# Reordering the small engines' work in a fused attention kernel that TensorE bounds

## The chip, the cores and the metric

The kernel runs on one core of a Trainium2 chip. The metric is the device time of one execution in microseconds. A core has five engines that run side by side, each working through its own queue: TensorE (PE in the profile, matrix products, with its weight loads as PEld), VectorE (DVE), ScalarE (ACT), GpSimd (POOL) and SyncE (SP). The last three also issue transfers (DMA). Matrix products are accumulated in PSUM[...] and are carried from there to SBUF by VectorE or ScalarE.

## The reference

A self-attention block on 16 images of 512 channels and 32 x 32 = 1024 positions, all in float32, with 4 heads of 128 channels:

```python
xg = x.reshape(b, 8, -1)
mu, var = mean(xg), var(xg)                       # group norm, 8 groups
xn = ((xg - mu) * rsqrt(var + 1e-5)).reshape(b, c, h, w) * gamma + beta
qkv = einsum('oc,bchw->bohw', qkv_w, xn) + qkv_b
q, k, v = to_heads(split(qkv, 3, axis=1))
attn = softmax(einsum('bhnd,bhmd->bhnm', q, k) * 128**-0.5)
out = einsum('bhnm,bhmd->bhnd', attn, v)
out = einsum('oc,bchw->bohw', proj_w, out) + proj_b
return x + out
```

## The kernel before

The kernel goes through the images b and the heads h of each, and in each head through eight steps j, one for each 128 key positions. A step has two halves of 512 query positions. In a half there are one score matmul `s`, the exponential `p` of it on ScalarE, and the weighted-sum matmul `po` of the step before. Between these, the other work of neighbouring images is laid in as "units": in head 0 the second half of the queries and keys (`qk`) of this image; in head 1 the output projection (`pp`) of the image before, and loading, statistics and normalisation of the next image; in head 2 the first half of `qk` of the next image; in head 3 its values (`v`).

```python
def scores(s, half):
    b, h, j = where(s)
    sc = ps_s.tile([P, HALF], F32, tag="s", name=f"s_{s}_{half}")        # two PSUM banks
    nc.tensor.matmul(sc, ks[b, h][:, ts(j, P)], qs[b, h][:, ts(half, HALF)], start=True, stop=True)
    ...
    nc.scalar.activation(ps[s][:, ts(half, HALF)], sc, AF.Exp, scale=SCALE)
    ...                                     # tot (a sum over the steps) on VectorE
```

Each 512 x 512 projection is done by Strassen's scheme with Winograd's sums, on two levels: seven outer products of seven inner ones. Outer sums of the right-hand side (`xt2`, `xt3`, `xt4`, and `t1` in place, in the profile the lines with L277) and inner sums (`qk_t`, `v_t`, `pp_t`, L518) are made on VectorE. One Strassen group keeps two PSUM banks, x and y. Products that share a bank are accumulated on top of each other, so a bank has to be copied out (`p1`, `u2`, `u3`) between two of them:

```python
def kept_copy(n):
    t[n] = upool.tile([P, HALF], F32, tag=n, bufs=1 if n == "u3" else 2, name=f"{name}_{n}")
    nc.scalar.copy(t[n][:, :width], t["x"][:, :width])                   # L448

def p1(): t["x"] = bank("x"); mm(t["x"], 1, True); kept_copy("p1")
def p2(): t["y"] = bank("y"); mm(t["y"], 2, True); out_("c11", t["y"], t["p1"])
def p6(): mm(t["x"], 6, False); kept_copy("u2")
def p5(): t["y"] = bank("y"); mm(t["y"], 5, True)
def p7(): mm(t["x"], 7, False); kept_copy("u3"); out_("c22", t["y"], t["u3"])
def p4(): mm(t["x"], 4, False); out_("c21", t["x"])
def p3(): mm(t["y"], 3, False); out_("c12", t["y"], t["u2"])
# out_: nc.scalar.copy (L565), or nc.vector.tensor_add (L567: qk_r, v_r, pp_r)
```

The sums over the keys (the denominators l) are made per head on VectorE from `tot`, and their reciprocals are written to a row in DRAM and read back, broadcast to all partitions, by two transfers that ScalarE's queue issues. A head's `po` is multiplied by them later (`divide`, L877).

```python
def denominators(b, h):
    tt = lpool.tile([P, N // BLK, BLK], F32, tag="tt", name=f"tt_{b}_{h}")
    nc.vector.transpose(tt.rearrange("p c m -> p (c m)"), t)             # L794
    nc.vector.tensor_reduce(part, tt, AX.X, ALU.add)                     # L796
    ...                                     # a few 32 x 32 operations, then reciprocal r
def spread_inverse(b, h, step):
    if step == 0: nc.scalar.dma_start(row..., inverse.pop((b, h)))       # L816
    else: nc.scalar.dma_start(rinv[b, h], rows_of.pop((b, h)).to_broadcast((P, N)))  # L821
```

The projection of the outputs adds to x again in tiles `y`, of which there are four buffers: each is loaded from x, has the product added (L752, L755), and is stored.

The order in which instructions stand on each engine comes from the framework's scheduler, which works from the program's order and from priorities; the loop is this:

```python
if 0 < s < steps and s % NB == 0:
    denominators(*where(s - 1)[:2])
for half in range(NH2):
    if s < steps:
        scores(s, half)
        if j == 1 and s > NB:
            spread_inverse(*where(s - NB)[:2], half)
        if half == 1 and j == 4 and s > NB:
            with tc.issue_after(added[b, h, 4].ins):
                divide(*where(s - NB)[:2])
    if s > 0:
        weighted_sum(s - 1, half)
    ...                                     # half of this step's units
```

Of the kernel before, what the change touches and what calls it, by code (L numbers as in the profile page):

```python
# [16 lines left out]
P = 128  # L17
# [5 lines left out]


LIMIT = 1e20


class Norm:
# [124 lines left out]
KC = 2  # L153
# [6 lines left out]
def fast_path(ctx, tc, x, sources, out, consts, flag, dims):  # L160
# [70 lines left out]
    def stats_chunk(b, c):  # L231
        if c == 0:
            mvs[b] = gn.tile([P, NCC, 2], F32, tag="mv", name=f"mv_{b}")
        if b == 0:
            norm.chunk(mvs[b], xs[b, c], c)
            return

        junk = lpool.tile([P, N], F32, tag="tt", name=f"junk_{b}_{c}")
        sums = gn.tile([P, 3], F32, tag="st", name=f"sums_{b}_{c}")
        nc.scalar.activation(junk, xs[b, c], AF.Identity, accum_out=sums[:, 0:1])  # L240
        nc.scalar.mul(mvs[b][:, c, 0:1], sums[:, 0:1], 1.0 / N)
        nc.scalar.mul(sums[:, 1:2], sums[:, 0:1], -1.0 / N)
        nc.scalar.activation(
            junk, xs[b, c], AF.Square, bias=sums[:, 1:2], accum_out=sums[:, 2:3]
        )
        nc.scalar.mul(mvs[b][:, c, 1:2], sums[:, 2:3], 1.0 / N)

    def stats_group(b):
        mu, sc = norm.group(mvs.pop(b))
# [20 lines left out]
            ]  # L270
        return b

    def sums_of_b(b, rows=(1, 2), chunks=range(KC)):

        def sub(o, i, j):
            for k in chunks:
                nc.vector.tensor_sub(b[o][k], b[i][k], b[j][k])  # L277

        if 1 in rows:
            sub("t1", "b12", "b11")  # L280
        if 2 in rows:
            sub("t2", "b22", "t1")
            sub("t3", "t2", "b11")
            sub("t4", "b21", "t2")

    def x_sums(b, rows=(1, 2)):
        if 1 in rows:
            xb[b] = halves([xs[b, c] for c in range(NCC)], "x")
        sums_of_b(xb[b], rows)
# [146 lines left out]
    def strassen(name, mm, out_, width=HALF):  # L436


        t = {}

        def bank(which):
            return ps_a.tile([P, HALF], F32, tag=which, name=f"{name}_{which}")

        def kept_copy(n):
            t[n] = upool.tile(
                [P, HALF], F32, tag=n, bufs=1 if n == "u3" else 2, name=f"{name}_{n}"
            )
            nc.scalar.copy(t[n][:, :width], t["x"][:, :width])  # L448
# [24 lines left out]
        def p4():  # L473
            mm(t["x"], 4, False)
            out_("c21", t["x"])

        def p3():
            mm(t["y"], 3, False)
            out_("c12", t["y"], t["u2"])

        units = {1: p1, 2: p2, 3: p3, 4: p4, 5: p5, 6: p6, 7: p7}
        return [units[i] for i in ORDER]

    def two_levels(name, site, b, blocks, finish, sums="make", homes="BBBB", prepare=None):
# [39 lines left out]
        def group_units(g):  # L524
            group = OUTER[g]
            n = len(group)
            have = haves[g]

            def weights():
                have["w"] = group_weights(site, g, b == 0 and site in range(PAIRS))  # L530

            def load(m):
                h = homes.find(homes[g], g + 1)
                if sums == "load" and h > 0:
                    nc.sync.dma_start(sum_tile(h, m), inner_kept[b, h, m])

            def inner_sum(m):
                if sums != "load" and m not in have:
                    make_sum(g, m)

            def inner(i, m):
                return inner_block(g, i, m)

            def mm(acc, j, first):
                an, bn = FACTORS[j]
                t, slot = SLOTS[an]
                for i in range(n):
                    nc.tensor.matmul(  # L548
                        acc[:, ts(i, Q)], have["w"][t][:, i, slot, :], inner(i, bn),
                        start=(first and i == 0), stop=True, skip_group_check=True,  # L550
                    )

            def out_(which, a, c=None):
                row, half = int(which[1]) - 1, int(which[2]) - 1
                if g not in R:
                    R[g] = rpool.tile(
                        [P, 2, 2, HALF], F32, tag=f"r{g % 3}", name=f"{name}_r{g}"
                    )
                dst = R[g][:, :n, row, ts(half, Q)]

                def view(t):
                    return t[:, : n * Q].rearrange("p (i q) -> p i q", q=Q)

                if c is None:
                    nc.scalar.copy(dst, view(a))  # L565
                else:
                    nc.vector.tensor_add(dst, view(a), view(c))  # L567
# [191 lines left out]


    ps, tot, po, rinv, last_eviction = {}, {}, {}, {}, {}
    inverse, rows_of, added = {}, {}, {}
    steps = B * HEADS * NB

    def where(s):
# [3 lines left out]
    def scores(s, half):  # L769
        b, h, j = where(s)  # L770
        sc = ps_s.tile([P, HALF], F32, tag="s", name=f"s_{s}_{half}")
        nc.tensor.matmul(  # L772
            sc, ks[b, h][:, ts(j, P)], qs[b, h][:, ts(half, HALF)], start=True, stop=True
        )
        if half == 0:
            ps[s] = ppool.tile([P, N], F32, tag="p", name=f"p_{s}")
        nc.scalar.activation(ps[s][:, ts(half, HALF)], sc, AF.Exp, scale=SCALE)  # L777
# [164 lines left out]
    def last_projection(b):  # L942
# [29 lines left out]
        sums_of_b(bl, (2,), (1,))  # L972
# [35 lines left out]
    def plan_head(b, h):  # L1008
# [9 lines left out]
        elif h == 1:  # L1018
# [4 lines left out]
            else:  # L1023
# [3 lines left out]
                for r in range(2):  # L1027
# [11 lines left out]
        elif b + 1 == B:  # L1039
# [3 lines left out]
            else:  # L1043
                os_[b, h] = opool.tile([P, N], F32, tag="o", name=f"o_{b}_{h}")
                plan[3].append(lambda: o_blocks(b))
                plan[3].append(lambda: sums_of_b(ob[b], (1,)))
                plan[5].append(lambda: sums_of_b(ob[b], (2,), (0,)))
# [42 lines left out]
    for s in range(steps + 1):  # L1090
        units = []
        if s < steps:
# [4 lines left out]
            if j == NB - 1 and h == 2 and b + 1 < B:  # L1097
                next_v.append(v_groups(b + 1))
                next_qk.append(qk_groups(b + 1, 1))
                units.append(ahead[f"v_{b + 1}"])  # L1100
        if 0 < s < steps and s % NB == 0:
            denominators(*where(s - 1)[:2])
        for half in range(NH2):
            if s < steps:
                scores(s, half)
                if j == 1 and s > NB:
                    spread_inverse(*where(s - NB)[:2], half)
                if half == 1 and j == 4 and s > NB:

                    with tc.issue_after(added[b, h, 4].ins):  # L1110
# [141 lines left out]
```

## Time and profile before

The time is 3247.06 us, the median of three runs (3245.63 to 3248.78). The profiled execution spanned 3251.7 us at a granted TensorE clock of 0.999. Groups of instructions that matter here, from the profile's groups (busy time is a union, the mean is that of one instruction):

| engine and line | what | count | mean, ns |
|---|---|---|---|
| TensorE L772 | score matmul s | 2048 records, two to a matmul | 594 |
| TensorE L548 | projection matmuls, 128 x 256 | 6076 records, two to a matmul | about 380 |
| ScalarE L777 | exponential p, 128 x 512 | 1024 | 596 |
| ScalarE L448 | copies p1, u2, u3 of qk, 128 x 512 | 288 | 585 |
| ScalarE L82 | normalise x, 128 x 512 | 124 | 807 |
| ScalarE L240, L243 | statistics, 128 x 1024 | 60 each | 1051, 1148 |
| ScalarE L241, L242, L246 | statistics, 128 x 1 | 60 each | 204, 190, 194 |
| VectorE L785 | tot, 128 x 1024 | 385 | 1222 |

A line of the timeline reads: start in us, duration in us, engine, source line, operation, output and inputs by the program's names, shapes, count; in brackets the time that the engine was idle before it and what ended the wait. TensorE's matmuls overlap, so what one costs is read from the distance between starts.

### The profile page before, as it was taken

The page shows a single profiled execution, that of the slowest core. Times are in us where ns is not written, and L with a number is a line of the kernel's source. Part 1 is how long each engine was busy: PE and PEld are TensorE (multiplying, and loading weights), DVE is VectorE, ACT ScalarE, POOL GpSimd, SP SyncE. Part 2 cuts the span into 40 slices and gives each one's busy share as a digit, 9 for nine tenths or more (in the row PEclk, how much of TensorE's full clock was granted, in tenths as well). Part 3 has the DMA queues.
Part 4 walks back from the last instruction along what each step waited for, and adds up shares of the span by engine and source line. Part 5 has one row for each costly group of instructions (what it writes and reads, how often), then busy time and mean ns, then how long its engine had stood idle before and what let it go on. Part 6 is the DMA issues. An engine that isn't in the chain of part 4 may idle for free.

```text
span 3251.7 us, 34056 instructions
## 1 busy us (share of the span) xinstructions
PE 3185.4 (98%) x10474; PEld 2178.0 (67%) x10474; DVE 2633.3 (81%) x4625; ACT 1439.8 (44%) x2709; POOL 516.3 (16%) x922
## 2 busy tenths in 40 slices
PE   8999999999999999999999999999999999999999
PEld 6566666766666766667666666666666666666664
DVE  8868878788787888878788787987879878788784
ACT  2534435354353543535435354353534535344442
POOL 0011121111211112111121111212012120121100
PEclk9999999999999999999999999999999999999999
DMA  5555553545545455454554545545455453555531
GB/s 161 186 192 164 180 172 123 186 153 182 172 142 181 145 194 161 161 161 146 187 162 162 169 132 193 164 165 167 136 180 171 164 173 134 182 160 172 181 124 40
DMA packets 209388, 526.92 MB, mean 162 GB/s; under 512 B 32816, under 2 KB 65840, under 8 KB 209200
## 3 DMA queue, kind: packets, MB, share of 16 engines
q1 hardware_dynamic: 128992, 276.88, 27.5%
q0 software_dynamic: 66240, 212.39, 19.5%
q10 hardware_dynamic: 13968, 35.41, 3.4%
q8 instruction: 86, 1.41, 0.2%
q14 instruction: 102, 0.84, 0.1%
HBM read 389.56 MB, written 135.00 MB: 161 GB/s over the span
## 4 chain that ended last, share of the span: by engine, by line
PE 47%; issue 27%; DVE 16%; DMA 7%; POOL 2%; ACT 1%; ACTq 0%; POOLq 0%; SPq 0%; DVEq 0%
PE po L867 13%; PE s L772 13%; PE qk_x L548 6%; PE qk_y L548 5%; PE pp_x L548 4%; DVE qk_t L518 3%; PE pp_y L548 3%; DMA vd<-vu 2%; DVE xt L277 2%; DMA out_y<-y 2%; DMA y<-in_x 2%; DMA v<-vd 1%; DVE qk_r L567 1%; DVE vu L703 1%; DVE tot L785 1%
## 5 line engine op out<-in xcount | busy, mean ns | idle before, releaser
L772 PE MATMUL s<-qk,qk 128*128 128x512 f32 x2048 | 1049.0, 594 | 4.5 <-ACT p L777 4.3
L867 PE MATMUL po<-p,v 128*128 128x512 f32 x2048 | 1053.2, 596 | 0.0
L777 ACT ACTIVATE p<-s 128x512 f32<-128x512 f32 x1024 | 610.0, 596 | 895.9 <-PE s L772 817.1
L867 PEld LDWEIGHTS po<-p,v 128*128 128x128 f32 x2048 | 602.0, 303 | 319.1 <-issue 202.3
L785 DVE TENSOR_TENSOR tot<-tot,p 128x1024 f32<-128x1024 f32 x385 | 470.4, 1222 | 147.9 <-ACT p L777 146.2
L772 PEld LDWEIGHTS s<-qk,qk 128*128 128x128 f32 x2048 | 387.0, 190 | 114.1 <-issue 43.5
L548 PE MATMUL qk_x<-qk_t,w 128*128 128x256 f32 x1344 | 356.8, 384 | 9.4 <-DVE qk_t L518 3.5
L548 PEld LDWEIGHTS qk_x<-qk_t,w 128*128 128x128 f32 x1344 | 250.2, 190 | 170.0 <-issue 66.2
L448 ACT COPY qk_u<-qk_x 128x512 f32<-128x512 f32 (+1 forms) x256 | 136.1, 532 | 262.2 <-PE qk_x L548 208.3
L711 POOL DMA_DIRECT2D vd<-vu x120 | 66.3, 552 | 992.4 <-DVE vu L703 990.7
L567 DVE TENSOR_TENSOR qk_r<-qk_y,qk_u 128x512 f32<-128x512 f32 (+1 forms) x256 | 158.3, 619 | 40.1 <-ACT qk_u L448 26.3
L548 PE MATMUL pp_x<-pp_t,w_proj 128*128 128x256 f32 x630 | 170.8, 388 | 6.7 <-ACT pp_p L448 6.7
L567 DVE TENSOR_TENSOR v_r<-v_y,v_u 128x512 f32<-128x512 f32 (+1 forms) x120 | 76.5, 638 | 112.2 <-ACT v_u L448 82.0
L548 PE MATMUL v_x<-v_t,w_v 128*128 128x256 f32 x630 | 166.7, 381 | 0.0
L522 POOL DMA_DIRECT2D kept_t<-qk_t x240 | 129.2, 540 | 233.4 <-DVE qk_t L518 188.7
L756 POOL DMA_DIRECT2D out_y<-y x120 | 66.2, 552 | 627.4 <-DVE y L755 595.2
L548 PEld LDWEIGHTS pp_x<-pp_t,w_proj 128*128 128x128 f32 x630 | 114.0, 190 | 76.4 <-issue 22.5
L548 PEld LDWEIGHTS v_x<-v_t,w_v 128*128 128x128 f32 x630 | 118.6, 190 | 55.2 <-issue 19.1
L716 POOL DMA_DIRECT2D v<-vd x240 | 140.0, 590 | 83.8 <-issue 60.0
L548 PE MATMUL qk_y<-x,w 128*128 128x256 f32 x512 | 143.5, 382 | 0.0
L448 ACT COPY v_u<-v_x 128x512 f32<-128x512 f32 (+1 forms) x124 | 66.2, 534 | 164.8 <-PE v_x L548 125.0
L646 DVE SCALAR_TENSOR_TENSOR qk<-qk_r,qkb_sb,qk_r 128x512 f32<-128x512 f32 x192 | 137.3, 743 | 1.6
(204 smaller groups left out, 4486.0 us busy)
## 6 DMA issues: line engine op xcount, KB each, us to landing
w<-kept SPq DMA_DIRECT2D x90, 512.0 KB, 4.1
kept_t<-qk_t POOLq DMA_DIRECT2D x180, 256.0 KB, 4.4
v_t<-kept_t SPq DMA_DIRECT2D x180, 256.0 KB, 3.0
w<-kept SPq DMA_DIRECT2D x90, 384.0 KB, 3.9
rinv<-row ACTq DMA_DIRECT2D x63, 512.0 KB, 5.4
x<-in_x POOLq DMA_DIRECT2D x60, 512.0 KB, 5.0
vd<-vu POOLq DMA_DIRECT2D x120, 256.0 KB, 3.4
v<-vd POOLq DMA_DIRECT2D x240, 128.0 KB, 4.6
```

The source lines that it names most:

```text
L448: nc.scalar.copy(t[n][:, :width], t["x"][:, :width])
L518: nc.vector.tensor_sub(to[:, i, :], inner_block(g, i, a), inner_block(g, i, c))
L522: nc.gpsimd.dma_start(t, to)
L548: nc.tensor.matmul(acc[:, ts(i, Q)], have["w"][t][:, i, slot, :], inner(i, bn), start=(first and i == 0), stop=True, skip_group_check=True,)
L567: nc.vector.tensor_add(dst, view(a), view(c))
L646: nc.vector.scalar_tensor_tensor(st[b, h][:, ts(half, HALF)], a, qkb_sb[:, i : i + 1], c, ALU.add, ALU.add)
L711: nc.gpsimd.dma_start(rows[which][ts(h, P), :], u)
L716: nc.gpsimd.dma_start(vs[b, pair][ts(q, BLK), half].rearrange("m h (k i) j -> m (h k) (i j)", k=n), rows[which].rearrange("(k m) (q e) -> ...
L772: nc.tensor.matmul(sc, ks[b, h][:, ts(j, P)], qs[b, h][:, ts(half, HALF)], start=True, stop=True)
L777: nc.scalar.activation(ps[s][:, ts(half, HALF)], sc, AF.Exp, scale=SCALE)
L785: added[b, h, j] = nc.vector.tensor_add(tot[b, h][:, i], tot[b, h][:, i], ps[s][:, i])
L867: nc.tensor.matmul(po[b, h][:, i], v_block(b, h, j), ps[s][:, i], start=(j == 0), stop=(j == NB - 1),)
```

## The change

Five things are changed, all of them in what the small engines do and when:

- The exponentials, the copies that empty PSUM banks, and the additions that do so (`out_`) are put under a raised scheduler priority, so that they are placed ahead of work that can wait.
- The two transfers of a head's reciprocals are issued behind the exponentials of the second halves of steps 1 and 2 (before: both in step 1).
- The outer sums of the next image are made near their use: t1 in head 1, xt2 at the start of head 2, xt3 and xt4 one step later (before: all in head 1). For the last image's outputs the split into rows 2 and 3 keeps the order as it was.
- The sums l of a head are made one step later, so that the transpose and the reduction don't stand at the head's start.
- The statistics of images 1 to 15 on ScalarE work on halves of 512 columns, with two more short operations that add the halves' sums.

```diff
+URGENT = 40
 ...
-        junk = lpool.tile([P, N], F32, tag="tt", name=f"junk_{b}_{c}")
-        sums = gn.tile([P, 3], F32, tag="st", name=f"sums_{b}_{c}")
-        nc.scalar.activation(junk, xs[b, c], AF.Identity, accum_out=sums[:, 0:1])
-        nc.scalar.mul(mvs[b][:, c, 0:1], sums[:, 0:1], 1.0 / N)
-        nc.scalar.mul(sums[:, 1:2], sums[:, 0:1], -1.0 / N)
+        def both(i, func, **kw):
+            for h in range(NH2):
+                junk = lpool.tile([P, HALF], F32, tag="tt", name=f"junk_{b}_{c}_{i}_{h}")
+                nc.scalar.activation(
+                    junk, xs[b, c][:, ts(h, HALF)], func, accum_out=sums[:, 2 * i + h][:, None], **kw)
+        both(0, AF.Identity)
         nc.scalar.activation(
-            junk, xs[b, c], AF.Square, bias=sums[:, 1:2], accum_out=sums[:, 2:3]
+            mvs[b][:, c, 0:1], sums[:, 0:1], AF.Identity, bias=sums[:, 1:2]
         )
-        nc.scalar.mul(mvs[b][:, c, 1:2], sums[:, 2:3], 1.0 / N)
+        nc.scalar.mul(neg, mvs[b][:, c, 0:1], -1.0 / N)
+        nc.scalar.mul(mvs[b][:, c, 0:1], mvs[b][:, c, 0:1], 1.0 / N)
+        both(1, AF.Square, bias=neg)
+        nc.scalar.activation(mvs[b][:, c, 1:2], sums[:, 2:3], AF.Identity, bias=sums[:, 3:4])
+        nc.scalar.mul(mvs[b][:, c, 1:2], mvs[b][:, c, 1:2], 1.0 / N)
 ...                                        # kept_copy
-            nc.scalar.copy(t[n][:, :width], t["x"][:, :width])
+            with tc.high_priority(URGENT):
+                nc.scalar.copy(t[n][:, :width], t["x"][:, :width])
 ...                                        # out_
-                if c is None:
-                    nc.scalar.copy(dst, view(a))
-                else:
-                    nc.vector.tensor_add(dst, view(a), view(c))
+                with tc.high_priority(URGENT):
+                    if c is None:
+                        nc.scalar.copy(dst, view(a))
+                    else:
+                        nc.vector.tensor_add(dst, view(a), view(c))
 ...                                        # scores
-        nc.scalar.activation(ps[s][:, ts(half, HALF)], sc, AF.Exp, scale=SCALE)
+        with tc.high_priority(URGENT):
+            exps[s] = nc.scalar.activation(ps[s][:, ts(half, HALF)], sc, AF.Exp, scale=SCALE)
 ...                                        # head 1, then head 2
-                    plan[6 + r].append(lambda r=r: x_sums(b + 1, (r + 1,)))
+                plan[6].append(lambda: x_sums(b + 1, (1,)))
 ...
+            plan[0].insert(2, lambda: x_sums(b + 1, (2,)))
+            plan[1].append(lambda: x_sums(b + 1, (3,)))
 ...                                        # the loop
-        if 0 < s < steps and s % NB == 0:
-            denominators(*where(s - 1)[:2])
+        if NB < s < steps and s % NB == 1:
+            denominators(*where(s - 2)[:2])
 ...
-                if j == 1 and s > NB:
-                    spread_inverse(*where(s - NB)[:2], half)
+                if j in (1, 2) and half == 1 and s > NB:
+                    with tc.issue_after(exps[s].ins):
+                        spread_inverse(*where(s - NB)[:2], j - 1)
```

More of the change, by code (lines that the diff above doesn't have):

```diff
@@ L236, in stats_chunk @@
             return
-        junk = lpool.tile([P, N], F32, tag="tt", name=f"junk_{b}_{c}")
-        sums = gn.tile([P, 3], F32, tag="st", name=f"sums_{b}_{c}")
-        nc.scalar.activation(junk, xs[b, c], AF.Identity, accum_out=sums[:, 0:1])
-        nc.scalar.mul(mvs[b][:, c, 0:1], sums[:, 0:1], 1.0 / N)
-        nc.scalar.mul(sums[:, 1:2], sums[:, 0:1], -1.0 / N)
+        sums = gn.tile([P, 2 * NH2 + 1], F32, tag="st", name=f"sums_{b}_{c}")
+        neg = sums[:, 2 * NH2 :]
+        def both(i, func, **kw):
+            for h in range(NH2):
+                junk = lpool.tile([P, HALF], F32, tag="tt", name=f"junk_{b}_{c}_{i}_{h}")
+                nc.scalar.activation(
+                    junk, xs[b, c][:, ts(h, HALF)], func, accum_out=sums[:, 2 * i + h][:, None],
+                    **kw,
+                )
+        both(0, AF.Identity)
         nc.scalar.activation(
-            junk, xs[b, c], AF.Square, bias=sums[:, 1:2], accum_out=sums[:, 2:3]
+            mvs[b][:, c, 0:1], sums[:, 0:1], AF.Identity, bias=sums[:, 1:2]
         )
-        nc.scalar.mul(mvs[b][:, c, 1:2], sums[:, 2:3], 1.0 / N)
+        nc.scalar.mul(neg, mvs[b][:, c, 0:1], -1.0 / N)
+        nc.scalar.mul(mvs[b][:, c, 0:1], mvs[b][:, c, 0:1], 1.0 / N)
+        both(1, AF.Square, bias=neg)
+        nc.scalar.activation(
+            mvs[b][:, c, 1:2], sums[:, 2:3], AF.Identity, bias=sums[:, 3:4],
+        )
+        nc.scalar.mul(mvs[b][:, c, 1:2], mvs[b][:, c, 1:2], 1.0 / N)
     def stats_group(b):
@@ L271, in halves, with sums_of_b @@
         return b
-    def sums_of_b(b, rows=(1, 2), chunks=range(KC)):
+    def sums_of_b(b, rows=(1, 2, 3), chunks=range(KC)):
         def sub(o, i, j):
@@ L282, in sums_of_b, with x_sums @@
             sub("t2", "b22", "t1")
+        if 3 in rows:
             sub("t3", "t2", "b11")
             sub("t4", "b21", "t2")
-    def x_sums(b, rows=(1, 2)):
+    def x_sums(b, rows=(1, 2, 3)):
         if 1 in rows:
@@ L761, in fast_path @@
     ps, tot, po, rinv, last_eviction = {}, {}, {}, {}, {}
-    inverse, rows_of, added = {}, {}, {}
+    inverse, rows_of, added, exps = {}, {}, {}, {}
     steps = B * HEADS * NB
@@ L971, in last_projection @@
         l, recip = last_division(b, HEADS - 1)
-        sums_of_b(bl, (2,), (1,))
+        sums_of_b(bl, (2, 3), (1,))
         for r in range(2):
@@ L1046, in plan_head @@
                 plan[3].append(lambda: sums_of_b(ob[b], (1,)))
-                plan[5].append(lambda: sums_of_b(ob[b], (2,), (0,)))
+                plan[5].append(lambda: sums_of_b(ob[b], (2, 3), (0,)))
         elif h == 2:
             spread(plan, staggered(qk_groups(b + 1, 0)), 0, NB)
+            plan[0].insert(2, lambda: x_sums(b + 1, (2,)))
+            plan[1].append(lambda: x_sums(b + 1, (3,)))
         else:
```

## The prediction

> **What bounds the kernel now.** I read the page's totals first, then TensorE's groups, then TensorE's waits, then the timeline of one typical image (image 5 of 16, 1055 to 1254 us).
>
> The first view is the page: its first line of totals, and in the groups of TensorE the two costliest.
>
> ```profile
> PE 3185.4 (98%) x10474; PEld 2178.0 (67%) x10474; DVE 2633.3 (81%) x4625; ACT 1439.8 (44%) x2709; POOL 516.3 (16%) x922
> ...
> L867 PE MATMUL po<-p,v 128*128 128x512 f32 x2048 | 1053.2, 596 | 0.0
> ```
>
> TensorE is busy 98%, so it sets the end, and only its idle gaps can be won. The record's own mean (596 ns) is not the price, since matmuls overlap; the spacing of starts in the timeline is. A 512-column matmul follows the last one after 0.86 us, a 256-column one after 0.43 us. There are 2048 of the first kind (scores and weighted sums) and 3038 of the second (projections): 2048 x 0.86 + 3038 x 0.43 = 1761 + 1306 = 3067 us, and about 65 us more for image 0's values, the last projection, small matmuls and the start. Added up start by start over the whole timeline, what exceeds this spacing is 105 us; 10.6 us of it lie before the first score. So 95 us, 2.9%, is the most that any reordering can win, and about 25 us of that are slips under 0.12 us each that I leave alone.
>
> The second view is who TensorE waited for: total us, times, longest.
>
> ```profile
> PE v_y L548 <- DVE v_r L567: 13.7, 30, 0.7
> ...
> PE qk_y L548 <- DVE qk_t L518: 8.5, 14, 1.3
> PE pp_x L548 <- ACT pp_p L448: 6.7, 14, 1.5
> PE s L772 <- ACT p L777: 4.3, 6, 2.3
> PE qk_x L548 <- DVE qk_t L518: 3.5, 15, 1.2
> PE qk_x L548 <- ACT qk_p L448: 3.5, 1, 3.5
> ```
>
> Most of these come 14 or 15 times, once or twice per image at the same place. In spacing, a typical image loses 0.2 to 1.2 us in its first block of eight steps (head 0), 1.06 in head 1, 1.6 to 4.6 in head 2, 1.66 in head 3. Image 0 is special: 2.7 in head 1 and 6.2 in head 2.
>
> The third view is the timeline around the two gaps of head 3 (VectorE and TensorE, image 5).
>
> ```profile
> 1239.63 1.25 DVE L877 TENSOR_TENSOR o<-o,rinv 128x1024 f32<-128x1024 f32 x1
> ...
> 1240.76 0.72 DVE L567 TENSOR_TENSOR v_r<-v_y,v_u 128x512 f32<-128x512 f32 x1
> ...
> 1241.54 1.13 PE L548 MATMUL v_y<-xt,w_v 128*128 128x256 f32 x4 [0.35 <-DVE v_r L567]
> ```
>
> The addition that empties PSUM (v_r) stands behind a division of 1.13 us that nobody needs yet. The second gap (0.56 us, at 1251.41) is the same with a transpose and a `vt` sum in front.
>
> [...]ScalarE sat 4.45 us before a copy at 1070.33, released by "DMA row<-r", because the rinv broadcast ahead of it waited for the row to land. [...]`row` (4 KB) took 1.3 to 6.4 us, median 2.3.[...]
>
> **The change part by part.** The changed kernel's instruction order on each engine can be read from its build, and is the same for images 1 to 14. I laid it over image 5's timeline.
>
> 1. Urgent emptying in head 3. The order now has v_r before the division, and the second v_r before a transpose (0.94) and a `vt` (0.60). The first is then done near 1240.3, wanted at 1240.6; the second near 1249.7, wanted at 1250.1. Both gaps go: in spacing 0.52 and 0.73, plus a 0.10 slip after each, is 1.4 us per image.
>
> 2. Urgent exponentials in head 1. Before, four normalisations (2.93 us) hold up an exponential and then the copy pp_p; TensorE waits 0.54. Now the exponential goes first, then two normalisations, then the copy, done near 1146.6 and wanted at 1147.1. But the later copy u3 now stands behind five normalisations and another exponential: laid out at 0.72 each it ends near 1151.9, and TensorE, which no longer lost 0.54, wants it at 1151.4. About 0.5 comes back. Net 0.2.
>
> 3. Outer sums where used, l's sums one block later (head 2). Before, the queue of VectorE at the head's start was:
>
> ```profile
> 1156.72 0.75 DVE L752 SCALAR_TENSOR_TENSOR y<-pp_r,projb_sb,y 128x512 f32<-128x512 f32 x1 [1.24 <-DMA y<-in_x]
> ...
> 1163.40 1.24 DVE L794 STREAM_TRANSPOSE tt<-tot 128x1024 f32<-128x1024 f32 x1
> ...
> 1164.56 0.38 DVE L518 TENSOR_TENSOR qk_t<-x 128x256 f32<-128x256 f32 x1
> ...
> 1165.09 0.67 PE L548 MATMUL qk_y<-qk_t,w 128*128 128x256 f32 x2 [0.42 <-DVE qk_t L518]
> ```
>
> Six outer sums (6 x 0.60 = 3.6) and the transpose (1.15) stood ahead of the inner sum qk_t. They move behind it. But the order of TensorE moves too: it wants qk_t1 at about 1159.4 instead of 1164.5, and qk_t1's second half is still behind the four y operations that wait for the load of y, which ends at 1156.7 (store 4.9 us, then load 3.3 us, on one buffer). They end near 1159.3, qk_t1 near 1159.65. So a wait of 0.3 to 0.7 remains there, and the rest of the head's 1.75 (0.58, 0.33, 0.21 before the first po, slips) mostly goes. Net 1.0.
>
> 4. Pinned broadcast. In head 0 the gap "s <- ACT p" (0.3 to 0.8 in about half of the images) follows the 4.45 us block above. The row is now issued one exponential later and the broadcast a step later, so the row has landed. Net 0.35 on average. Image 15 loses 1.7 us to a late qk_u copy; I count 1.0 of it as won.
>
> 5. Statistics in halves. Per chunk, seven ScalarE instructions (1051 + 1148 + 2 x 190 + 3 x 196 = 3.17 us) become thirteen: 2 x 596 + 2 x 706[...] + 4 x 190 + 5 x 196 = 4.34; [...]+0.6 us per chunk, 2.4 per image. In images 1 to 14 the statistics ended at 1126.4 and TensorE wants their mean at 1136.7, so it costs nothing there.
>
> 6. Image 0. Here no projection fills TensorE, and the order now puts the mean's matmul (pm) right behind the score whose exponential stands ahead of the last statistics: after that score come 0.6 exponential, 0.6 half, three short ones and the mean, so TensorE should stand about 1.9 us. The eight normalisations still run in one block (5.75 us) ahead of an exponential: 2.3 us lost before, about 3.5 now. Against this the 3.54 us behind the row's landing should shrink to about 1.6. Sum: 5.8 before, 7.0 now; 1 us worse, with v's 1.4 won.
>
> Sum: 14 x (1.4 + 0.2 + 1.0 + 0.35) = 41; image 0 +0.4; image 15 +1.0; together 42 us. Part 2 shows a removed wait that is partly met by the next one, so I take off 5 for those I have not seen. 3247 - 37 = 3210 us, 1.1% less.
>
> **The rivals.** First: TensorE's gaps close and only move on, because VectorE (45.0 of 51 us busy in head 2) is nearly full there and the load of y sets when its queue comes free. For it: the 1.24 us wait on DMA, which in images 7 and 11 is longer (gaps of 1.5 and 1.8 us on xt). Against it: heads 3 and 0 do not depend on y. Then only 14 x 1.7 is won: 3222 us. Second: the urgent exponentials push PSUM copies and normalisations back, and p7's matmul, now one matmul behind p6's, waits for u2 in head 2; with 0.5 to 1 us per image lost anew the gain is 25 us or less, 3225 to 3235, and with a few long ScalarE waits none. Third: everything closes, including the slips, 3247 - 75 = 3172; the slips have no queue entry in front of them, so I give this little.
>
> **Range and chances.** The middle is 3210. The first two rivals reach up to 3235, the full closing of all the gaps listed down to about 3192. Range 3193 to 3236. Faster by over 2% needs under 3182, 65 of the 95 us: 0.04. Slower by over 2% would need 65 us of new gaps: 0.01. Within 2%: 0.95.
>
> **What would show it.** In the profile after: "v_y <- v_r" gone from TensorE's waits (part 1); "pp_x <- ACT" about as large, but on u3 rather than p (2); in head 2 one wait on qk_t, directly behind the y operations (3); "s <- ACT p" gone outside image 0 (4); ScalarE busy about 30 us more, with TensorE's busy time unchanged (5); a wait of pm on the mean of about 2 us in image 0 (6). If head 2 keeps 1.7 us or more per image, part 3 was wrong; if a wait on an activation copy shows up 14 times or more with over 0.5 us, the second rival was right.

## The result, and the profile after

The changed kernel takes 3205.18 us, the median of four runs (3202.90 to 3209.22); the kernel before took 3247.92 beside it (3245.63 to 3251.33). The ratio is 0.9869, with a 95% interval of 0.9852 to 0.9886: 43 us, 1.3% less. The prediction was 3210, in a range of 3193 to 3236.

The page of the changed kernel, first line of totals. In this kernel the exponential is L797, the score matmul L791, the weighted sum L887, the projection matmul L566, the kept copy L466, `out_` L584 and L586, the outer sums L293 and the inner ones L536.

```profile
PE 3160.6 (99%) x10474; PEld 2182.9 (68%) x10474; DVE 2634.4 (82%) x4625; ACT 1503.3 (47%) x3069; POOL 527.9 (16%) x922
```

TensorE's busy time fell by 25 us with the same number of instructions; the prediction had it unchanged. The reason is in the records: one lasts about 0.16 us longer than the distance to the start of the next (592 ns against 429, 379 against 215), so the first 0.16 us of every late start counts as busy, and there are fewer late starts. A wait in the profile is for the same reason 0.16 us shorter than the loss in spacing. VectorE has the same work; ScalarE has 63.5 us more, where the prediction expected about 30. Then whom TensorE waited for, in the changed kernel (total us, times, longest):

```profile
PE pm L52 <- DVE mean L50: 11.4, 2, 10.8
PE pp_x L566 <- ACT pp_u L466: 5.7, 14, 0.4
PE qk_y L566 <- DVE qk_t L536: 4.9, 5, 2.2
PE s L791 <- ACT p L797: 4.1, 1, 4.1
PE qk_x L566 <- ACT qk_u L466: 3.0, 3, 1.6
```

The biggest line of before, v_y on v_r (13.7 us, 30 times), is gone. Of the waits that came in every image only pp_x is left, now on a copy u (the third one, u3) instead of p. The wait of s on p is left once, in image 0.

I added up, start by start, what TensorE's spacing exceeds 0.86 us (512 columns) or 0.43 us (256 columns), as for the prediction. Per image, mean of images 1 to 14, and the single images, in us:

| stretch | before | after | won | predicted |
|---|---|---|---|---|
| head 0 | 0.59 | 0.23 | 0.35 | 0.35 |
| head 1 | 1.17 | 0.95 | 0.22 | 0.2 |
| head 2 | 2.28 | 0.79 | 1.49 | 1.0 |
| head 3 | 1.66 | 0.31 | 1.36 | 1.4 |
| images 1 to 14 | 79.8 | 31.9 | 47.9 | 41 |
| image 0 | 11.0 | 8.9 | 2.1 | 0.4 |
| image 15 | 3.9 | 4.7 | -0.9 | 1.0 |
| up to the first score | 10.6 | 8.9 | 1.7 | 0 |

That is 105.3 before, 54.4 after, 50.9 won, against 50.6 between the two profiled spans (3251.7 and 3201.1). The medians are 42.7 apart: the profiled run of before (3253.5 us) lies 5.6 us above its median and that of the changed kernel (3202.9) 2.3 us below, so the table overstates the gain by 8 us.

The timeline of the changed kernel in head 3 of image 5 shows the first of the two gaps closed:

```profile
1223.93 0.72 DVE L586 TENSOR_TENSOR v_r<-v_y,v_u 128x512 f32<-128x512 f32 x1
...
1224.54 1.25 DVE L897 TENSOR_TENSOR o<-o,rinv 128x1024 f32<-128x1024 f32 x1
...
1224.90 1.03 PE L566 MATMUL v_y<-xt,w_v 128*128 128x256 f32 x4
```

The emptying now stands before the division, ends at 1224.65, and the matmul carries no bracket: it did not wait. In head 1 of the same image:

```profile
1136.18 0.58 ACT L797 ACTIVATE p<-s 128x512 f32<-128x512 f32 x1
...
1136.66 0.81 ACT L85 ACTIVATE x<-x,sh,sc 128x512 f32<-128x512 f32 x1
1137.37 0.36 ACT L466 COPY pp_u<-pp_x 128x256 f32<-128x256 f32 x1
...
1137.78 0.48 PE L566 MATMUL pp_x<-pp_t,w_proj 128*128 128x256 f32 x1 [0.41 <-ACT pp_u L466]
```

The third copy still stands behind a normalisation and an exponential, and TensorE waits 0.41 us for it (0.57 in spacing). In head 2:

```profile
1142.15 1.58 DVE L771 SCALAR_TENSOR_TENSOR y<-pp_r,projb_sb,y 128x512 f32<-128x512 f32 x2
...
1143.65 1.29 DVE L774 TENSOR_TENSOR y<-y,pp_r 128x512 f32<-128x512 f32 x2
...
1144.85 0.41 DVE L536 TENSOR_TENSOR qk_t<-x 128x256 f32<-128x256 f32 x1
```

The sum qk_t is directly behind the four y operations. In this image it is nearly in time; in five of the images the load of y lands later, the four operations wait for it, and TensorE waits for qk_t.

### The profile page after: what moved, and what is told of

It reads as the page before. It is cut to its first block, busy times and chain, and to the rows that moved or that the text cites. A ratio compares the mean times of both kernels' runs of the same rounds, so it can differ in the third digit from the quotient of the medians.

```text
span 3201.1 us, 34401 instructions
## 1 busy us (share of the span) xinstructions
PE 3160.6 (99%) x10474; PEld 2182.9 (68%) x10474; DVE 2634.4 (82%) x4625; ACT 1503.3 (47%) x3069; POOL 527.9 (16%) x922
## 4 chain that ended last, share of the span: by engine, by line
PE 86%; DVE 6%; issue 3%; DMA 2%; ACT 2%; POOL 1%; SPq 0%; ACTq 0%; POOLq 0%; DVEq 0%
PE po L887 24%; PE s L791 24%; PE qk_x L566 12%; PE qk_y L566 8%; PE v_x L566 6%; PE v_y L566 4%; PE pp_x L566 4%; PE pp_y L566 3%; ACT x L85 2%; DMA y<-in_x 1%; DVE pp_r L633 1%; POOL rstd L67 1%; DVE pp_r L586 1%; DVE tot L805 1%; DVE o L897 1%
## 5 line engine op out<-in xcount | busy, mean ns | idle before, releaser
L791 PE MATMUL s<-qk,qk 128*128 128x512 f32 x2048 | 1047.8, 593 | 4.1 <-ACT p L797 4.1
L887 PE MATMUL po<-p,v 128*128 128x512 f32 x2048 | 1050.6, 595 | 0.0
L797 ACT ACTIVATE p<-s 128x512 f32<-128x512 f32 x1024 | 610.8, 597 | 934.7 <-PE s L791 893.0
L887 PEld LDWEIGHTS po<-p,v 128*128 128x128 f32 x2048 | 602.9, 303 | 316.2 <-issue 210.3
L791 PEld LDWEIGHTS s<-qk,qk 128*128 128x128 f32 x2048 | 387.7, 190 | 92.0 <-issue 29.4
L566 PEld LDWEIGHTS qk_x<-qk_t,w 128*128 128x128 f32 x1344 | 250.1, 190 | 177.1 <-issue 77.4
L566 PE MATMUL qk_x<-qk_t,w 128*128 128x256 f32 x1344 | 357.7, 383 | 4.4 <-ACT qk_u L466 3.0
L466 ACT COPY qk_u<-qk_x 128x512 f32<-128x512 f32 (+1 forms) x256 | 136.3, 532 | 230.8 <-PE qk_x L566 228.8
L586 DVE TENSOR_TENSOR qk_r<-qk_y,qk_u 128x512 f32<-128x512 f32 (+1 forms) x256 | 157.9, 617 | 40.0 <-ACT qk_u L466 26.0
L566 PE MATMUL pp_x<-pp_t,w_proj 128*128 128x256 f32 x630 | 169.4, 385 | 5.9 <-ACT pp_u L466 5.7
L586 DVE TENSOR_TENSOR v_r<-v_y,v_u 128x512 f32<-128x512 f32 (+1 forms) x120 | 75.8, 631 | 110.6 <-ACT v_u L466 80.3
L566 PE MATMUL v_x<-v_t,w_v 128*128 128x256 f32 x630 | 166.6, 381 | 0.0
L566 PEld LDWEIGHTS pp_x<-pp_t,w_proj 128*128 128x128 f32 x630 | 115.5, 190 | 73.0 <-issue 25.6
L566 PEld LDWEIGHTS v_x<-v_t,w_v 128*128 128x128 f32 x630 | 118.4, 190 | 55.3 <-issue 19.1
L566 PE MATMUL qk_y<-x,w 128*128 128x256 f32 x512 | 142.2, 379 | 0.0
L466 ACT COPY v_u<-v_x 128x512 f32<-128x512 f32 (+1 forms) x124 | 66.3, 535 | 160.1 <-PE v_x L566 130.1
```

The lines of the kernel that those rows point to most:

```text
L566: nc.tensor.matmul(acc[:, ts(i, Q)], have["w"][t][:, i, slot, :], inner(i, bn), start=(first and i == 0), stop=True, skip_group_check=True,)
L797: exps[s] = nc.scalar.activation(ps[s][:, ts(half, HALF)], sc, AF.Exp, scale=SCALE)
L887: nc.tensor.matmul(po[b, h][:, i], v_block(b, h, j), ps[s][:, i], start=(j == 0), stop=(j == NB - 1),)
```

## The experiments

All times are medians. The kernel before, run beside them, took 3245.7 us in the first four, 3246.2 in the next four and 3246.3 in the last; ratios are to it, with 95% intervals. "The changed kernel" is 3205 us throughout; it was run again beside the last four alone (experiment 12).

**1. The priority of the emptying alone, taken out of the changed kernel.**

```diff
-                with tc.high_priority(URGENT):
-                    if c is None: ...                   # out_: scalar.copy or vector.tensor_add
+                if c is None: ...
```

> The changed kernel with the raised priority taken from out_ alone (the additions and copies that empty PSUM banks into r). My theory: head 3's two gaps come back, because v_r stands behind the division and behind a transpose and a vt sum again: TensorE's gaps in head 3 go from 0.29 to about 1.65 us per image, all else stays, 15 x 1.36 = 20 us slower than the changed kernel, about 3225 us. Rival: head 3 was freed by moving the sums l and the outer sums off VectorE's queue, and the priority of out_ matters little: head 3 stays at 0.3 us, 3205 us.

3231.0 us, ratio 0.995 (0.9933 to 0.9967): 26 us above the changed kernel. In TensorE's waits of this run the old line is back, as large as it was (13.7, 30 times):

```profile
PE v_y L566 <- DVE v_r L585: 13.6, 30, 0.8
```

Head 3 loses 1.66 us per image again (1.35 x 14 = 19), head 2 0.4 more. Step 1 of the prediction, 1.4 us per image, is thereby shown.

**2. Both kinds of sums back where they were.** Outer sums all in head 1, l at the start of the head.

```diff
-        if NB < s < steps and s % NB == 1: denominators(*where(s - 2)[:2])
+        if 0 < s < steps and s % NB == 0: denominators(*where(s - 1)[:2])
-                plan[6].append(lambda: x_sums(b + 1, (1,)))       # and two inserts in head 2
+                for r in range(2): plan[6 + r].append(lambda r=r: x_sums(b + 1, ((1,), (2, 3))[r]))
```

> The changed kernel with the outer sums back in head 1 and the sums l back at the head's start; priorities, pinned broadcast and statistics in halves stay. My theory: head 2's gaps come back, because the inner sum qk_t stands behind six outer sums and the transpose: from 0.33 us (most images) to about 1.5 per image, 14 x 1.2 = 17 us slower, about 3222 us; heads 0, 1 and 3 as in the changed kernel. Rival: the priorities alone freed head 2, by the earlier last product of the output projection: head 2 stays near 0.4 us, 3205 to 3208 us.

3219.7 us, ratio 0.9914 (0.9897 to 0.993): 14.5 us above the changed kernel. Head 2 of images 1 to 14 goes from 0.79 back to about 1.45 us, not to the 2.28 of before, so less than half of its gain hangs on the place of the sums; the rest of the 14.5 us lies in head 1, image 0 and image 15. Experiment 6 parts the two kinds.

**3. Both transfers where they were, without a pin.**

```diff
-                if j in (1, 2) and half == 1 and s > NB:
-                    with tc.issue_after(exps[s].ins):
-                        spread_inverse(*where(s - NB)[:2], j - 1)
+                if j == 1 and s > NB:
+                    spread_inverse(*where(s - NB)[:2], half)
```

> The changed kernel with both transfers of the reciprocals issued in step 1 again, unpinned (the order of TensorE is the same). My theory: ScalarE's queue waits for the reciprocals and then for the row to land before it goes on, and because the sums l are made a step later this is longer than it was: a gap on an exponential or a copy in head 0 in most images, and perhaps in heads 2 and 3; 0.5 to 2 us per image, 8 to 30 us slower, 3213 to 3235 us. Rival: the waits on ScalarE are covered by the two banks of scores, nothing changes: 3205 us.

3276.9 us, ratio 1.0094 (1.0077 to 1.0111): slower than the kernel before, and 72 us above the changed one. Both theories were far off. The gaps lie in head 0 of images 1 to 14 (4.95 us on average instead of 0.23). ScalarE and TensorE in the timeline of this run, image 6:

```profile
1268.40 0.32 ACTq L836 DMA_DIRECT2D row<-r  x1
...
1273.05 0.33 ACTq L841 DMA_DIRECT2D rinv<-row  x1
1273.42 0.59 ACT L466 COPY qk_u<-qk_x 128x512 f32<-128x512 f32 x1 [4.00 <-DMA row<-r]
...
1274.06 1.48 PE L566 MATMUL qk_x<-qk_t,w 128*128 128x256 f32 x4 [3.29 <-ACT qk_u L466]
```

The broadcast that reads the row stands in ScalarE's queue ahead of the copy qk_u, and is issued 4.65 us after the row, when that has landed. The copy waits 4.0 us with it, and TensorE 3.3 us behind the copy. This comes 14 times (45 us). The other 20 us and more are mostly a slower TensorE after the wait (granted clock 0.50 from 1276 to 1278 us), which the last section shows.

**4. Statistics at full width.**

```diff
-        both(0, AF.Identity) ...                         # thirteen instructions on halves
+        nc.scalar.activation(junk, xs[b, c], AF.Identity, accum_out=sums[:, 0:1]) ...   # seven
```

> The changed kernel with the statistics on full 1024 columns as before. My theory: the halves cost ScalarE 2.4 us per image and bring TensorE nothing in images 1 to 14, so the gaps stay as they are (0.22, 0.91, 0.33, 0.29 us in heads 0 to 3), ScalarE's busy time falls by about 60 us, and image 0's wait for the mean (0.8 us) shrinks by some tenths: 3204 to 3206 us. Rival: a full-width instruction of 1.1 us delays an exponential or a bank copy, and head 1 gains a gap of 0.3 us or more per image: 3209 us or more.

3200.0 us, ratio 0.9854 (0.9838 to 0.9871), 5 us less than the changed kernel with overlapping intervals; the two profiled runs are level (3203.4 and 3202.9). ScalarE is busy 59.6 us less (1443.7 instead of 1503.3), and TensorE's gaps in images 1 to 14 are about the same. So the halves bring nothing here. What is less is head 2 of image 0 (2.3 us instead of 6.75), where the normalisations now come in blocks of four, one and three with exponentials between, instead of eight at once.

**5. The kernel before with the emptying's priority alone.** The reverse of experiment 1.

```diff
+                with tc.high_priority(URGENT):                     # URGENT = 40
                     if c is None: ...                             # out_
```

> The kernel before with one part of the change alone: the copies and additions that empty the projections' PSUM get the raised priority; everything else is as before. Taking that priority out of the changed kernel cost 26 us. If the emptying has its own gaps (head 3's two waits of v_y on v_r) that no other part touches, the kernel before should gain nearly the same: 15 x 1.4 = 21 us by the prediction's step, up to 26 by the removal; 3220 to 3227 us. Rival: the parts support one another (the addition can only be early because the sums no longer fill VectorE); then it gains under 10 us, 3236 or more, and head 3 keeps a part of its 1.66 us.

3311.8 us, ratio 1.02 (1.0176 to 1.0225): 66 us slower, against both theories. Head 3 is won (0.3 instead of 1.7), but head 0 takes 5.1 us per image and head 2 3.8 (before 0.6 and 2.3). ScalarE in head 0 of image 5, first in the kernel before, then in this run:

```profile
1065.30 0.58 ACT L448 COPY qk_u<-qk_x 128x512 f32<-128x512 f32 x1
...
1069.96 0.33 ACTq L821 DMA_DIRECT2D rinv<-row  x1
1070.33 0.58 ACT L448 COPY qk_p<-qk_x 128x512 f32<-128x512 f32 x1 [4.45 <-DMA row<-r]
```

```profile
1082.16 0.33 ACTq L825 DMA_DIRECT2D rinv<-row  x1
1082.53 0.58 ACT L451 COPY qk_u<-qk_x 128x512 f32<-128x512 f32 x1 [2.33 <-DMA row<-r]
```

In the kernel before, ScalarE stands still for 4.45 us as well, but the copy that TensorE wants first happens to be ahead of the broadcast. The priority of other instructions moved it behind. Waiting of this kind was nearly free in one order, and in the other head 0 loses 4.5 us more per image.

**6 and 7. l early, with and without the pin.** Outer sums as in the changed kernel.

```diff
-        if NB < s < steps and s % NB == 1: denominators(*where(s - 2)[:2])
+        if 0 < s < steps and s % NB == 0: denominators(*where(s - 1)[:2])    # 6 and 7
-                if j in (1, 2) ... issue_after ...
+                if j == 1 and s > NB: spread_inverse(*where(s - NB)[:2], half)   # 7 alone
```

> The changed kernel with the denominator sums l back at the start of the head, outer sums where the change put them, both transfers still pinned. Putting the sums of both kinds back cost 14.5 us. If it was l's transpose ahead of the inner sum, this run loses most of that again, 3212 to 3219 us, and head 2 shows 0.6 us or more per image. If it was the outer sums, it stays within 3 us of the changed kernel, 3203 to 3208.

3222.3 us, ratio 0.992 (0.9904 to 0.9937): 17 us above the changed kernel, as much as experiment 2. So it is the place of l that counts, and that of the outer sums makes no difference that these runs can show. About 9 of the 17 us lie in head 2 of images 1 to 14 (1.44 us instead of 0.79), the rest in head 1, image 0 and image 15.

> As the run with l early and pinned, but both transfers where the kernel before had them, without a pin. Unpinning them with l late cost 72 us, with ScalarE waiting 14 times for the row to land in front of a PSUM copy (45 us) and TensorE at half rate after most of these waits. Theory: the pin is only needed because l comes a block later, so that the row is written when its reader is next in ScalarE's queue; with l early the row is written 6 us sooner, and this run costs 0 to 10 us more than the pinned one with l early, 3212 to 3225 us. Rival: the pin is worth 60 to 70 us by itself; then 3270 or more.

3287.3 us, ratio 1.0125 (1.0108 to 1.0142): the rival was right. My theory that the pin is needed only because l comes later falls. With l early or late, leaving the pin out costs 65 to 72 us, once the emptying has its priority.

**8. The changed kernel with a higher priority and two more pins.**

```diff
-URGENT = 40
+URGENT = 150
+ # x's chunk 3: normalise issued after the head's last exponential
+ # image 15: last_bias issued after an exponential of head 2
```

> The changed kernel with three edits aimed at the gaps that its trace still shows: the raised priority goes from 40 to 150, so that the last copy of head 1 (u3) comes ahead of the normalisations; the last chunk's normalisation is issued behind the head's last exponential; in image 15 the bias addition that waits for the load of y is issued behind an exponential of head 2. If u3's place sets head 1's 0.57 us and the queue behind the bias addition image 15's 2.3 us, it gains 14 x 0.57 + 2.3 + 2 to 5 in image 0, 12 to 15 us: 3190 to 3194 us. Rival: the gap moves on to the next copy or to VectorE's sums; then 3200 to 3206.

3215.5 us, ratio 0.9899 (0.9882 to 0.9915): 10 us slower than the changed kernel. The aimed-at gaps shrank in image 0 (4.1 us instead of 8.9) and image 15 (2.1 instead of 4.7). Head 1 won only 0.1 of 0.57, because TensorE then waited for VectorE's pp_r in the same place. Head 2 lost 1.7 us per image (whether by the higher priority or by the late normalisation was not parted), in a new line of TensorE's waits:

```profile
PE qk_x L566 <- DVE qk_t L536: 23.7, 12, 3.4
```

**9. As 5, with the pin of the change.**

```diff
+                with tc.high_priority(URGENT): ...                 # out_, as in 5
+                if j in (1, 2) and half == 1 and s > NB:
+                    with tc.issue_after(exps[s].ins):
+                        spread_inverse(*where(s - NB)[:2], j - 1)
```

> The kernel before with two parts of the change: the raised priority for emptying the projections' PSUM, and both transfers pinned behind the second exponential of steps 1 and 2. With the priority alone the kernel took 3312 us: head 3 won its 1.4 us per image, but head 0 went from 0.2-1.2 to about 5 us, since the copy qk_u now stands behind the transfer that waits for the row (46 us in all on ScalarE, and TensorE at half rate after most of it), and head 2 from 1.7 to 3.8. If that transfer is the cause in head 0, the pin gives back 15 x 4.7 = 70 us and touches nothing else: 3242 us, 3236 to 3250, which is no better than the kernel before, as head 2's loss (about 2.1 per image) eats head 3's gain. Rival: the wait moves to another copy behind the same transfer; then head 0 keeps over 2 us per image, and it takes 3270 or more.

3245.3 us, ratio 1.0 (0.9991 to 1.0009). Head 0 is back at 0.23 us per image, 66 us in all, and head 2 keeps its 3.5: as expected, the two parts together bring nothing. ScalarE still waits for the row, as its waits in this run show, but before a copy out of PSUM that nobody is waiting for:

```profile
ACT qk_r L569 <- DMA row<-r: 27.2, 15, 2.8
```

**10. The changed kernel without the priority of exponentials and kept copies.**

```diff
-            with tc.high_priority(URGENT):
-                nc.scalar.copy(t[n][:, :width], t["x"][:, :width])
+            nc.scalar.copy(t[n][:, :width], t["x"][:, :width])     # and the exponential likewise
```

> The changed kernel without the raised priority of the exponentials and of the kept copies (p and u); the emptying keeps it. By the prediction's step 2 this part is worth 0.2 us per image, since the wait on p only moved to u3: 3205 + 14 x 0.2 = 3208 us, 3203 to 3213, head 1 at about 1.1 us. Rival: as with the emptying, the priority decides on which side of a transfer a copy stands, and its absence costs far more, 3225 or more.

3259.4 us, ratio 1.0043 (1.0027 to 1.006): 54 us above the changed kernel, where I expected 3. Head 1 is not worse (0.74 instead of 0.95); head 2 takes 4.45 us instead of 0.79, which is 51 us over fourteen images: about 35 are longer waits on qk_t, the rest mostly the slower TensorE that the last section shows (mean granted clock 0.994, in the changed kernel 0.999). (The profiled run, 3250.1 us, was the fastest of the four, 47 us above that of the changed kernel.) TensorE's waits in this run, VectorE's timeline in head 2 of image 5, then GpSimd's and SyncE's before it:

```profile
PE qk_y L565 <- DVE qk_t L535: 39.8, 14, 4.1
```

```profile
1159.12 0.75 DVE L770 SCALAR_TENSOR_TENSOR y<-pp_r,projb_sb,y 128x512 f32<-128x512 f32 x1 [0.95 <-DMA y<-in_x]
...
1160.99 0.41 DVE L535 TENSOR_TENSOR qk_t<-x 128x256 f32<-128x256 f32 x1
```

```profile
1148.84 1.15 POOL L774 DMA_DIRECT2D out_y<-y  x2 [5.69 <-DVE y L773]
...
1153.76 0.54 POOL L757 DMA_DIRECT2D y<-in_x  x1 [2.19 <-DMA out_y<-y]
```

```profile
1148.81 0.32 SPq L379 DMA_DIRECT2D w<-kept  x1
```

The same in the changed kernel, GpSimd and then SyncE:

```profile
1134.92 1.15 POOL L775 DMA_DIRECT2D out_y<-y  x2 [5.69 <-DVE y L774]
...
1138.21 1.18 POOL L758 DMA_DIRECT2D y<-in_x  x2 [0.55 <-DMA out_y<-y]
```

```profile
1133.53 0.32 SPq L379 DMA_DIRECT2D w<-kept  x1
```

The load of y needs a buffer, and that comes free when a store of y has landed (the load at 1153.76 waited 2.19 us for it). In the changed kernel the load follows the store after 3.3 us, without the priority after 4.9. Then the load comes later, the y operations stop VectorE's queue for it (0.95 us at 1159.12), and the inner sum qk_t behind them is late. This holds beyond image 5: in experiment 10 the load is issued 0.8 to 1.6 us after the start of head 2 in all of images 1 to 14, in the changed kernel 0.9 to 1.6 us before it in all but image 7. The next weights (512 KB) are issued 1.4 us ahead of the store in the changed kernel, and at the same moment here. They are at the same moment in experiments 5 and 9 too, where the load follows after 5.0 us and head 2 takes 3.5 to 3.8, and nearly so in the kernel before (0.14 us ahead, 4.9). Whether the weights are what slows the store was not shown: it was not tried alone, and in some images of the changed kernel (image 7: 5.0 us) the load follows as late without it.

**11 and 12. Two late pins, and the changed kernel again beside it.** As 8, but with the priority at 40 and the normalisation moved in image 0 alone.

```diff
+ # image 0: the next image's chunk 3 normalised after the head's last exponential
+ # image 15: last_bias issued after an exponential of head 2
```

> The changed kernel with two edits, the priority left at 40: in image 0 the last chunk's normalisation is issued behind the head's last exponential (images 1 to 14 stay as they are), and in image 15 the bias addition that waits for the load of y is issued behind an exponential of head 2. In the run that had these edits together with the higher priority, image 0 lost 4 us instead of 9 and image 15's head 0 0.2 instead of 3.2; the 10 us that it lost all lay in head 2 of images 1 to 14, which these edits do not touch. So 5 + 3 = 8 us less than the changed kernel on the same chip, 6 to 9: about 3197 us. Rival: image 0's and 15's gaps reappear a few steps later; then within 2 us of it.

> The changed kernel itself on the same chip, to be compared with the run of two late pins: 3205 us, 3200 to 3209.

3202.4 us, ratio 0.9867 (0.985 to 0.9883), and 3205.0, ratio 0.9877 (0.986 to 0.9893): 2.6 us of the expected 8, not apart by their intervals. Image 15 did win 5.5 us in the profiles (1.6 instead of 7.1); image 0 won 0.6 instead of 5, since the exponentials there still wait behind six normalisations. Head 2 lost 4 us in all, in three or four images with a late load of y. Those images differ between two executions of the same kernel as well, so whether the edit has a part in it stays open. Nothing that was run is clearly faster than the changed kernel; full-width statistics together with the late bias addition were not tried.

## Why the prediction held, point by point

- **Part 1, the emptying, 1.4 us per image:** right. The table has 1.36, and experiment 1 takes it away again.
- **Part 2, urgent exponentials, net 0.2:** near for head 1 in the two finished kernels (0.22), with the wait moved from p to u3 as predicted (0.57 in spacing, 0.5 expected); but without this priority head 1 lost no more (0.74), so these runs do not show that it is worth anything there. What the prediction missed is that the same priority holds head 2 together: without it the load of y comes later and 51 us are lost there (experiment 10).
- **Part 3, head 2, net 1.0:** the remaining wait is where it was said to be, directly behind the y operations. The term was too small, 1.49, because I let the y operations end as late as before. In the changed kernel the load of y is issued 1.4 us before the head starts (image 5; before: 0.1), and in nine of the fourteen images head 2 then loses under 0.6 us. So part 3 had the wrong owner for more than half of this gain: the place of the sums gives about 0.65 of the 1.49 (experiments 2 and 6, and of the two moves that of l shows all the effect), and in experiment 2, too, the load of y is issued 1.2 us or more before the head in ten of the fourteen images. The earlier load goes with the priority of part 2.
- **Part 4, the pin, 0.35 us in head 0:** right as a difference of the two kernels, wrong as the worth of the part. Experiments 3, 5, 7 and 9 give 65 to 72 us: the emptying's priority puts qk_u behind the broadcast, and the pin undoes that. I read the block of 4.45 us in the profile of before as harmless, since TensorE hardly waited, and did not ask what would stand behind it after the reordering.
- **Image 15, +1.0:** wrong, the term that failed with its sign. ScalarE and TensorE in the changed kernel:

```profile
3033.95 1.15 ACT L956 ACTIVATE y<-y,projb_sb 128x1024 f32<-128x1024 f32 x1 [3.62 <-DMA y<-in_x]
...
3035.62 1.13 PE L566 MATMUL qk_x<-qk_t,w 128*128 128x256 f32 x4 [1.63 <-ACT qk_u L466]
```

The copy is again late, but it stands behind the last bias addition, which waits for its own load. Pinned behind an exponential of head 2 (experiments 8 and 11), head 0 of image 15 falls to 0.2 us.

- **Part 5, statistics, 0.6 us per chunk and free:** free for images 1 to 14, but the size was off: 63.5 us more over 60 chunks is 1.06. By their rows the durations grew by 1.47 per chunk, not 1.17: the first halves take 626 ns (596 was put in), and the two sums of halves, L253 and L259, 286 and 294 (196 was put in). The overlap of neighbouring instructions gave back 0.41; the prediction's step from 1.17 to 0.6 counts on 0.57, which no trace showed. (Its sign, "about 30 us more", was also less than its own 60 x 0.6 = 36.) Experiment 4 takes 59.6 us away and loses nothing.
- **Part 6, image 0, 7.0 us of three waits:** the pm wait was 0.8 in spacing, not 1.9, the third (1.6) did not occur, and the block of eight normalisations cost 4.1 and not 3.5, and then 1.8 more, as the last section shows. In sum 2.1 won instead of 0.4.
- **The rivals:** waits that only move, and a wait on the copies, were both real possibilities: they are what most of the runs with one part left out or added show (3220 to 3312 us). In the full change little of them is left: late loads of y in five images, as the first rival said, and the wait on u3 in head 1, 14 times and 0.41 us long at most in the profile's waits (0.57 in spacing), where the second rival's sign was over 0.5. That everything closes did not happen: 54 us of gaps remain.
- **The sum:** 42 less 5, so 37, against 42.7 measured. That this is so near is partly luck: part 3 and image 0 gave more than was put in and image 15 less, and in the profiles the gain is 50.9. (The split of the span in the prediction's first step, 3067 + 65 + 105, is also 15 us short of 3252; nothing rests on it.) Above all, the parts do not add up one by one. Taken out singly, the emptying, the other priorities, the pin and l are worth 26, 54, 72 and 17 us: 169 together, four times the gain of the whole. Put in singly, the first costs 66, and with the pin it brings nothing. My working came near the total because it compared two finished orders, not because each part has its own worth.

## What to carry to other kernels

When a change is a set of reorderings, compare the finished orders on each engine, and don't expect a part to show its worth alone: try each part by taking it out of the whole as well as by putting it into the old kernel. Here a transfer whose issue waited for an earlier one held up the copy behind it in its engine's queue, 4.45 us in the kernel before and 4.00 in experiment 3; look for such blocks even where they cost nothing now, and pin them behind something late. Where a bound engine waits for a sum, follow the queue ahead of that sum down to the transfer and the buffer that it waits for.

## What the runs showed of the hardware

Some waits of TensorE cost more than their length: the matmuls after them ran at a granted clock of 0.50 for a while. In image 0 of the changed kernel, ScalarE and TensorE in the timeline:

```profile
150.89 5.75 ACT L85 ACTIVATE x<-x,sh,sc 128x512 f32<-128x512 f32 x8
...
157.17 1.79 PE L791 MATMUL s<-qk,qk 128*128 128x512 f32 x2 [4.14 <-ACT p L797]
158.75 1.91 PE L887 MATMUL po<-p,v 128*128 128x512 f32 x2
```

A pair of these took 1.02 us before the wait. Busy times of the same run in two stretches (after the five engines: the granted clock, the DMA share, GB/s):

```profile
157.50:160.91 3.41, 3.41 (x6) 1.22 (x5) 3.41 (x7) 1.17 (x3) 1.25 (x3) 0.50 0.99 329
160.91:164.00 3.09, 3.09 (x15) 2.57 (x14) 3.03 (x10) 0.91 (x2) 1.08 (x2) 1.00 1.02 396
```

The granted clock is 0.50 for 3.41 us, 512-column matmuls start 0.85 us apart instead of 0.43, and 1.8 us are lost on top of the wait. The kernel before has one such stretch, also 3.41 us long at 0.50 and from 170.81 us on, 0.5 us after the end of a wait of 3.54 us. Apart from a stretch at the program's end these are the only ones in the two traces: the other waits after the first score, up to 2.27 us before and 2.20 after, were not followed by one. Which waits are followed by one is not settled by so few.

In experiment 3 the same is seen behind the wait of 3.29 us shown there:

```profile
1274.06 1.48 PE L566 MATMUL qk_x<-qk_t,w 128*128 128x256 f32 x4 [3.29 <-ACT qk_u L466]
1275.32 1.92 PE L791 MATMUL s<-qk,qk 128*128 128x512 f32 x2
1277.03 1.57 PE L887 MATMUL po<-p,v 128*128 128x512 f32 x2
1278.43 0.60 PE L566 MATMUL qk_y<-x,w 128*128 128x256 f32 x2
```

```profile
1274.00:1276.00 2.00, 1.95 (x5) 1.38 (x6) 1.66 (x2) 1.37 (x4) 0.45 (x1) 0.68 0.99 299
1276.00:1278.00 2.00, 2.00 (x4) 0.79 (x3) 0.25 (x1) 0.81 (x2) 2.00 (x5) 0.50 0.74 240
1278.00:1280.00 2.00, 2.00 (x10) 1.58 (x9) 0.50 (x1) 0.00 (x0) 0.46 (x1) 0.97 0.98 193
```

From 1274.06 to 1278.43 it takes 4.37 us for what takes 3 x 0.86 = 2.58 elsewhere: 1.8 us lost. Over the 14 waits this makes 25 us, an estimate from this one, and with the 45 of the waits 70 of the 72 us that unpinning costs. The mean granted clock of the runs agrees: it is 0.992 in experiment 3 and 0.999 in the changed kernel, and 0.007 of 3274 us is 23 us. It is 0.992 in experiment 5 too, and 0.994 in experiment 10 (0.005 of 3248 us is 16).
